# Softplus as one function, eight load buffers and column groups kept together in a four-layer convolution and state-space kernel

## The chip, the cores and the metric

The kernel runs on one core of a Trainium2 chip. The core has five engines with an instruction queue each, worked off in order: TensorE (PE; its weight loads are shown apart as PEld), VectorE (DVE), ScalarE (ACT), GpSimd (POOL) and SyncE (SP), which here only issues DMAs. The metric is the device time of one execution in microseconds. All data are float32.

## The reference

Eight images of 384 channels and 32 x 32 pixels go through four layers. Layer 0 is a two-way selective state-space layer (Mamba) beside a small convolution, layer 1 a block with a depthwise convolution, linear attention and an MLP, layer 2 a sum of large depthwise convolutions, layer 3 a pointwise and a 13 x 13 depthwise convolution with GELU. The change touches layer 0 and, through a shared helper, layer 1. Of layer 0, for a sequence of 1024 pixels in either direction:

```python
u = silu(causal_conv4(u) + conv1d_b)
dt, Bm, Cm = split(u @ x_proj_w.T, [24, 40])
delta = softplus(dt @ dt_proj_w.T + dt_proj_b)
h = exp(delta * A) * h + (delta * u) * Bm      # per channel and each of 16 states, step by step
y = sum(h * Cm over the 16 states) + u * D
y = y * silu(z)
```

## The kernel before

The program is written with a tile framework: the author writes operations on tiles from pools with a fixed number of buffers, in a trace order; a scheduler then orders each engine's instructions by priority (earlier in the trace first) and by its own estimate of when inputs and buffers are ready, and the program with its semaphore waits is fixed from there on. Each engine's order is that of the built program.

**Stages.** `_layers01` runs the `front` of image 0 alone, then for each image b the state recurrence `scan(b)`, into which it deals out pieces of `front(b + 1)` and of `layer1(b - 1)` by quotas; in the first scan a weight folding, and later the preparation of the large convolutions' kernels, run beside it. After the last scan come the rest of `layer1(7)` and the large convolutions of layers 2 and 3, which the change leaves alone.

**The scan.** 12 units (direction, half of the sequence, block of 128 channels) of 4 rounds each. A round does 4 of the 16 states: a tile's 128 partitions hold 32 channels x 4 states, and two tiles `hs` of 1024 columns hold the block's 128 channels. Per tile: ACT makes `da`, the exponential of delta times A, in two halves (L776); DVE multiplies delta u with B (`du`, L781) and runs two scans (L793); POOL multiplies with C (L802). The function `sums` (L732), two rounds later, adds the four states of each channel on PE: four products, each with a 32-column selection matrix `selt`, write to the four 32-partition strips of one PSUM tile `acc` (L736). There are eight `hs` buffers and four `da` buffers. Delta and delta u come from DRAM through SP's queue into `rep` tiles (six buffers).

**Column groups.** The same form, products with 32 output columns at four places of the array, is in `col32` (L507 to L514, its product is L511): it does the depthwise 3 x 3 convolutions of layer 0 (`lc`) and layer 1 (`dw`), by `conv3`, with three taps, and the causal convolution (`c`, from the `ut` loads) with one. Each of its four strips reads a tile loaded from DRAM, tag `im`, six buffers. The projection `xd` (L652) has two groups of 64 columns.

**Softplus.** For each of three channel blocks and either direction, PE multiplies `dt` (L667) into PSUM; ACT makes softplus(a) as relu(a) + ln(1 + exp(-|a|)): Abs (L671) and Relu (L672) read PSUM with the bias, then Exp (L676) and Ln (L678) run on the first result. The addition is on DVE in `deltas` (L683), a piece that is put off by one step; it also forms delta u (L684) in the other temporary, sends both to DRAM by POOL's queue (L685, L686), adds u of both directions in the place of the first (L687) and scales it by D (L689). `t2` is the pool of 128 x 512 temporaries, eleven buffers; `uc` tiles are of the tag `a6`, seven buffers.

ACT evaluates functions from a table that holds a set of them; ACT_TABLE_LOAD rows in the profile are the exchanges of that set.

Of the kernel before, what the change touches and what calls it, by code (L numbers as in the profile page):

```python
# [1 line left out]

# [7 lines left out]
AF = mybir.ActivationFunctionType  # L10
# [6 lines left out]
NC = C // P  # L17
H = 32
W = 32
L = H * W  # L20
HALF = 512
# [12 lines left out]
NR = NST // 4  # L34
IMG = (H + 2) * (W + 2)

N_A6, N_T2, N_S2, N_W, N_IM = 7, 11, 3, 4, 6
N_REP, N_DA, N_HS = 6, 4, 8
TP = H * (KP // 2)
PADW = KS // 2  # L40
HIMG = H // 2 * (W + 2)
# [333 lines left out]
def _layers01(tc, nc, B, xv, x2_d, dram, ident, mean_w, eps5, eps6, one, half, minus1, vec, bns, bnt,  # L375
# [12 lines left out]
    with ExitStack() as ctx:  # L388
# [26 lines left out]
        dlv = dl_d.rearrange("b d (c p) l -> b d p c l", p=P)  # L415
        vv = v_d.rearrange("b d (c p) l -> b d p c l", p=P)
# [7 lines left out]
        wx = const(xproj_t.rearrange("(k p) e -> p k e", p=P), [P, NC, 64], "wx")  # L424
# [9 lines left out]
        selt = const(sel, [P, 32], "selt")  # L434
# [27 lines left out]
        def t2(name):  # L462
            return sp.tile([P, HALF], FP, tag="t2", name=name, bufs=N_T2)
# [17 lines left out]
        late = []  # L481
# [22 lines left out]
                    start=(k == 0), stop=(k == NC - 1),  # L504
                )

        def col32(ps, lhs, rhs, taps):  # L507

            for i in range(taps):
                for j in range(4):  # L510
                    nc.tensor.matmul(  # L511
                        ps[32 * j : 32 * j + 32, :], lhs(j, i), rhs(j, i),
                        start=(i == 0), stop=(i == taps - 1), skip_group_check=True,
                    )  # L514

        def rows(t):
            return t.rearrange("p (h w) -> p h w", w=W)
# [13 lines left out]

        def conv3(t_d, slot, h, c, taps, name, psum=psum):

            ims = []
            for j in range(4):
                im = sp.tile([P, 18 * (W + 2)], FP, tag="im", name=f"{name}_i{j}", bufs=N_IM)
                src = bass.AP(
                    t_d.tensor, t_d[slot, 32 * (4 * c + j), 16 * h * (W + 2)].offset,
                    [[IMG, 32], [1, 3], [1, 18 * (W + 2) - 2]],
                )  # L540
                nc.sync.dma_start(im[:96, 0 : 18 * (W + 2) - 2], src)
                ims.append(im.rearrange("p (h w) -> p h w", w=W + 2))
            ps = psum(name)
            col32(
                ps, lambda j, i: taps[:96, (4 * c + j) * 3 + i, :],
                lambda j, i: ims[j][:96, i : i + 16, 0:W], 3,
            )
            return ps

# [22 lines left out]
        def front(b):  # L572

            xn = []
            for h in range(2):
# [7 lines left out]
                t, mid = image6(f"xn_{b}_{h}")  # L583
# [42 lines left out]
            for h in range(2):  # L626
                cols = bass.ts(h, HALF)
                ucs = [a6(f"uc_{b}_{h}_{d}") for d in range(2)]
                for c in range(NC):
                    uts = []  # L630
                    for j in range(4):
                        ut = sp.tile([P, 18 * (W + 2)], FP, tag="im", name=f"ut_{b}_{h}_{c}_{j}", bufs=N_IM)
                        src = bass.AP(
                            u_d.tensor, u_d[b % 2, 32 * (4 * c + j), h * HALF].offset,
                            [[UL, 32], [1, 4], [1, HALF + 3]],
                        )
                        nc.sync.dma_start(ut[:, 0 : HALF + 3], src)
                        uts.append(ut)
                    for d in range(2):
                        ps = psum(f"c1_{b}_{h}_{c}_{d}")  # L640
                        col32(
                            ps, lambda j, i: t1[:, d * NG + 4 * c + j, :],
                            lambda j, i: uts[j][:, 3 * d : 3 * d + HALF], 1,
                        )
                        nc.scalar.activation(ucs[d][:, c, :], ps, AF.Silu, bias=vec("conv1d_b", c))
                    yield 2

                xd = t2(f"xd_{b}_{h}")
                ps = psum(f"xd_{b}_{h}")
                for k in range(NC):  # L650
                    for d in range(2):
                        nc.tensor.matmul(  # L652
                            ps[64 * d : 64 * d + 64, :], wx[:, k, :], ucs[d][:, k, :],
                            start=(k == 0), stop=(k == NC - 1), skip_group_check=True,
                        )
                nc.scalar.copy(xd, ps)
                for d in range(2):
                    lo = 64 * d + DTR
                    nc.scalar.dma_start(bc_d[b, d][:, cols], xd[lo : lo + 2 * NST, :])
                yield 3  # L660

                for c in range(NC):
                    dls, ts = [], []
                    for d in range(2):
                        ps = psum(f"dt_{b}_{h}_{d}_{c}")
                        at = slice(64 * d, 64 * d + DTR)
                        nc.tensor.matmul(  # L667
                            ps, wdt[at, c * P : (c + 1) * P], xd[at, :], start=True, stop=True
                        )
                        t, dl = t2(f"sp_{b}_{h}_{d}_{c}"), t2(f"dl_{b}_{h}_{d}_{c}")  # L670
                        nc.scalar.activation(t, ps, AF.Abs, bias=vec("dt_b", c))  # L671
                        nc.scalar.activation(dl, ps, AF.Relu, bias=vec("dt_b", c))  # L672
                        ts.append(t)
                        dls.append(dl)
                    for t in ts:
                        nc.scalar.activation(t, t, AF.Exp, scale=-1.0)  # L676
                    for t in ts:
                        nc.scalar.activation(t, t, AF.Ln, bias=one)  # L678

                    def deltas(h=h, c=c, dls=dls, ts=ts, ucs=ucs):  # L680
                        for d in range(2):
                            dl, t = dls[d], ts[d]
                            nc.vector.tensor_add(dl, dl, t)  # L683
                            nc.vector.tensor_mul(t, dl, ucs[d][:, c, :])  # L684
                            nc.gpsimd.dma_start(dlv[b, d][:, c, bass.ts(h, HALF)], dl)  # L685
                            nc.gpsimd.dma_start(vv[b, d][:, c, bass.ts(h, HALF)], t)  # L686
                        nc.vector.tensor_add(ucs[0][:, c, :], ucs[0][:, c, :], ucs[1][:, c, :])  # L687
                        ud = t2(f"ud_{b}_{h}_{c}")
                        nc.scalar.activation(ud, ucs[0][:, c, :], AF.Copy, scale=vec("D", c))  # L689
                        nc.scalar.dma_start(udv[b][:, c, bass.ts(h, HALF)], ud)  # L690

                    defer(1, deltas)
                    yield 3

        def scan(b):
# [5 lines left out]
            late = []  # L701
# [27 lines left out]
                    ts.append(t)  # L729
                return ts  # L730

            def sums(k, r, hs, acc, y0, zt):  # L732
                d, h, c = units[k]
                cols = bass.ts(h, HALF)
                for j in range(4):
                    nc.tensor.matmul(  # L736
                        acc[32 * j : 32 * j + 32, :], selt, hs[j // 2][:, bass.ts(j % 2, HALF)],
                        start=(r == 0), stop=(r == NR - 1), skip_group_check=True,
                    )
                if r == 0:  # L740
                    nc.tensor.matmul(acc, ident, y0, start=False, stop=False, skip_group_check=True)
                if r < NR - 1:
                    return
                if d == 0:
                    yt = s2(f"yt_{b}_{h}_{c}")
                    nc.scalar.copy(yt, acc)
                    nc.scalar.dma_start(yfv[b][:, c, cols], yt)
                else:
                    nc.vector.tensor_mul(zt, acc, zt)
                    nc.gpsimd.dma_start(gv[b][:, c, cols], zt)  # L750
# [3 lines left out]
            acc = y0 = zt = nxt = None  # L754
            for k, (d, h, c) in enumerate(units):
                cols = bass.ts(h, HALF)
                second = k % (2 * NC) >= NC
                for r in range(NR):
                    if r == 0:
                        acc = accp.tile([P, HALF], FP, tag="acc", name=f"acc_{b}_{d}_{h}_{c}")  # L760
                        y0 = s2(f"y0_{b}_{d}_{h}_{c}")
# [3 lines left out]
                        nc.sync.dma_start(zt, zv[b][:, c, cols])  # L765
                    if r == 1 and k + 1 < len(units):
                        nxt = [load(k + 1, 0)]
                    hs = []
                    way = slice(None) if d == 0 else slice(None, None, -1)
                    end = HALF - 1 if d == 0 else 0  # L770
                    for i in range(2):
# [25 lines left out]
                        if not second:  # L797
# [4 lines left out]
                        nc.gpsimd.tensor_mul(  # L802
                            pairs(t), pairs(t), bct[r][:, 1:2, :].to_broadcast([P, 2, HALF])
                        )
                        hs.append(t)
                    late.append((k, r, hs, acc, y0, zt))
# [407 lines left out]
```

## Time and profile before

| | us |
|---|---|
| median of 10 runs | 5787.8 (5779.2 to 5796.4) |
| the profiled execution | 5790.1, span 5788.3 |
| front of image 0, alone | 0 to 215 |
| eight scans with what is dealt into them | 215 to 4630 |
| rest of layer 1 for image 7 | 4630 to about 4980 |
| large convolutions | about 4980 to 5788 |
| busy: PE / DVE / ACT / POOL | 4819 / 3676 / 3065 / 2898 |
| of ACT: 776 table loads of 1283 ns | 996 |

The mean granted clock of TensorE is 0.897 of full speed; in the first scan it is 0.70. Busy times are shares of stages with different limits, so they are read by stage. In the rows of groups, the count and the mean of one instruction stand first, then the idle time of the engine just before it and what ended it. A product in float32 leaves two records on PE.

### The profile page before, as it was taken

To read this page: it belongs to the slowest core of one execution; us is meant where nothing else is said; L and a number is where in the kernel's file an instruction comes from. 1 tells how busy PE (TensorE), PEld (TensorE's weight loads), DVE (VectorE), ACT (ScalarE), POOL (GpSimd) and SP (SyncE) were. 2 spreads that over 40 slices of the span, in tenths; PEclk is the share of its full clock that TensorE was granted. 3 is DMA by queue.
4 is the path that set the end of the run, shared out by engine and by line. 5 is a ranking of instruction groups with operands and counts; after the bars stand their busy time and mean duration, and the time that the engine had idled before them with its cause. 6 is when DMAs were issued, how large, how long until landed. Compare 5 with 4: busy or idle time off the path is not lost. (4 is left out here: it accounts for less than half of the span.)

```text
span 5788.3 us, 57844 instructions
## 1 busy us (share of the span) xinstructions
PE 4819.3 (83%) x19550; PEld 2105.0 (36%) x19550; DVE 3676.0 (64%) x3775; ACT 3064.8 (53%) x4116; POOL 2898.2 (50%) x1603
## 2 busy tenths in 40 slices
PE   5576579977988799879988997899778869899999
PEld 1121124322332243223323332333233324598498
DVE  0399997868687768786878786878678801011211
ACT  1656546774567567846784687468645613000211
POOL 3276676557554656564656564656466700110133
PEclk7677689988999899889998998999889979999999
DMA  9555475677567756764566467546644541366676
GB/s 299 187 183 174 144 251 186 229 194 217 187 210 202 216 171 192 166 208 133 186 206 191 140 177 191 186 140 178 180 143 131 127 95 49 91 170 158 194 166 150
DMA packets 528255, 1012.16 MB, mean 175 GB/s; under 512 B 60616, under 2 KB 196248, under 8 KB 527960
## 3 DMA queue, kind: packets, MB, share of 16 engines
q1 hardware_dynamic: 387952, 665.99, 38.1%
q0 software_dynamic: 71136, 248.53, 16.4%
q10 hardware_dynamic: 68872, 93.95, 5.2%
q8 instruction: 155, 2.54, 0.2%
q14 instruction: 140, 1.15, 0.1%
HBM read 763.86 MB, written 288.36 MB: 182 GB/s over the span
## 5 line engine op out<-in xcount | busy, mean ns | idle before, releaser
L802 POOL TENSOR_TENSOR hs<-hs,bct 128x1024 f32<-128x1024 f32 x768 | 2380.7, 3101 | 1171.1 <-DVE hs L793 662.2
L776 ACT ACTIVATE da<-dlt,neg_a 128x512 f32<-128x512 f32 x1536 | 1032.4, 714 | 849.0 <-DVE hs L793 761.3
L793 DVE TENSOR_TENSOR_SCAN hs<-da,carry,du 128x512 f32<-128x512 f32 x768 | 947.0, 1268 | 449.5 <-PE acc L736 213.0
L781 DVE TENSOR_TENSOR du<-vr,bct 128x1024 f32<-128x1024 f32 x768 | 1044.7, 1360 | 41.3 <-issue 16.6
L793 DVE TENSOR_TENSOR_SCAN hs<-da,du 128x512 f32<-128x512 f32 x768 | 901.2, 1208 | 153.3 <-ACT da L776 73.6
L736 PE MATMUL acc<-hs,selt 128*32 128x512 f32 x3072 | 737.8, 675 | 300.5 <-POOL hs L802 247.5
L1064 PE MATMUL mo<-hm,w 128*128 128x512 f32 x1152 | 566.2, 632 | 82.4 <-ACT hm L1062 61.3
L502 PE MATMUL mf<-ln,w 128*128 128x512 f32 x1152 | 543.3, 612 | 33.3 <-ACT dl L672 32.3
L736 PEld LDWEIGHTS acc<-hs,selt 128*32 128x32 f32 x3072 | 124.8, 115 | 727.5 <-POOL hs L802 395.7
L1064 PEld LDWEIGHTS mo<-hm,w 128*128 128x128 f32 x1152 | 215.9, 198 | 427.5 <-issue 257.0
L776 ACT ACT_TABLE_LOAD x265 | 340.0, 1283 | 38.1 <-DVE hs L793 26.1
L502 PEld LDWEIGHTS mf<-ln,w 128*128 128x128 f32 x1152 | 214.2, 194 | 346.5 <-issue 284.3
L316 PE MATMUL cv_b<-xt_b,toep 128*64 128x256 f32 x2688 | 304.8, 388 | 14.1 <-DVE xt_b L298 14.1
L316 PE MATMUL cv_a<-xt_a,toep 128*64 128x256 f32 x2688 | 305.8, 389 | 9.1 <-DVE xt_a L298 9.1
L502 PE MATMUL in<-xn,win 128*128 128x512 f32 x576 | 292.6, 640 | 22.8 <-ACT phi_k L874 21.9
L511 PE MATMUL dw<-dw_i,t3b 96*32 96x512 f32 x1152 | 234.9, 718 | 81.3 <-DMA dw_i<-h_d 81.3
L316 PEld LDWEIGHTS cv_b<-xt_b,toep 128*64 128x64 f32 x2688 | 282.5, 199 | 36.7 <-issue 16.3
L316 PEld LDWEIGHTS cv_a<-xt_a,toep 128*64 128x64 f32 x2688 | 282.8, 199 | 31.7 <-issue 11.3
L511 PE MATMUL lc<-lc_i,t 96*32 96x512 f32 x1152 | 224.6, 685 | 52.5 <-issue 28.6
L511 PE MATMUL c<-ut,t 128*32 128x512 f32 x768 | 193.6, 677 | 50.5 <-DMA ut<-u_d 38.8
L502 PE MATMUL op<-g,wo 128*128 128x512 f32 x288 | 143.4, 649 | 81.1 <-DMA g<-g_d 54.9
L1062 ACT ACTIVATE hm<-mf,biasf 128x512 f32<-128x512 f32 x192 | 130.6, 687 | 146.6 <-PE mf L502 145.0
(189 smaller groups left out, 5635.1 us busy)
## 6 DMA issues: line engine op xcount, KB each, us to landing
dlt<-dl_d SPq DMA_DIRECT2D x384, 256.0 KB, 4.4
vr<-v_d SPq DMA_DIRECT2D x384, 256.0 KB, 4.6
bct<-bc_d SPq DMA_DIRECT2D x256, 256.0 KB, 4.1
ut<-u_d SPq DMA_DIRECT2D x192, 257.5 KB, 4.9
lc_i<-xn_d SPq DMA_DIRECT2D x192, 228.8 KB, 4.8
dw_i<-h_d SPq DMA_DIRECT2D x192, 228.8 KB, 4.1
tp_d<-g_d POOLq DMA_DIRECT2D x64, 672.0 KB, 7.7
w<-w_d SPq DMA_DIRECT2D x64, 576.0 KB, 5.6
```

The costliest lines, as they stand in the source:

```text
L316: nc.tensor.matmul(ps[2 * H * e : 2 * H * (e + 1), 0:BW], tp[:, 2 * (g % (GB // 2)) + e, :, :, t].rearrange("p c j -> p (c j)"), rhs, star ...
L502: nc.tensor.matmul(ps, w[:, k, m * P : (m + 1) * P], rhs[k] if isinstance(rhs, list) else rhs[:, k, :], start=(k == 0), stop=(k == NC - 1),)
L511: nc.tensor.matmul(ps[32 * j : 32 * j + 32, :], lhs(j, i), rhs(j, i), start=(i == 0), stop=(i == taps - 1), skip_group_check=True,)
L736: nc.tensor.matmul(acc[32 * j : 32 * j + 32, :], selt, hs[j // 2][:, bass.ts(j % 2, HALF)], start=(r == 0), stop=(r == NR - 1), skip_group ...
L776: nc.scalar.activation(da[:, bass.ts(j, HALF)], dlt[:, bass.ts(j, HALF)], AF.Exp, scale=neg_a[:, g, r : r + 1],)
L781: nc.vector.tensor_mul(pairs(du), pairs(vt), bct[r][:, 0:1, :].to_broadcast([P, 2, HALF]),)
L793: nc.vector.tensor_tensor_scan(t[:, s][:, way], da[:, s][:, way], du[:, s][:, way], k_c if second else 0.0, ALU.mult, ALU.add,)
L802: nc.gpsimd.tensor_mul(pairs(t), pairs(t), bct[r][:, 1:2, :].to_broadcast([P, 2, HALF]))
L1062: nc.scalar.activation(hm, ps, AF.Gelu, bias=biasf[:, NC * i + f, :])
L1064: nc.tensor.matmul(acc[m], wb[:, f, m * P : (m + 1) * P], hm, start=(i == 0 and f == 0), stop=(i == FF // C - 1 and f == NC - 1),)
```

## The change

Three things:

- Softplus is one activation on ACT, from PSUM with the bias, into `dl`; Abs, Relu, Exp, Ln and DVE's addition go.
- `t2` has nine buffers, `im` has eight. Delta u is written over u in `uc` (and sent from there), the sum of both directions is formed first, in a `t2` tile of its own.
- A helper `together` takes a list of products. The first gets a scheduling edge without a semaphore behind all that makes their inputs (`made`: the loads, the last Silu, or POOL's two products); the others follow at raised priority and in program order. It is used for `col32`, for `xd` and for the four products of `sums`.

```diff
-N_A6, N_T2, N_S2, N_W, N_IM = 7, 11, 3, 4, 6
+N_A6, N_T2, N_S2, N_W, N_IM = 7, 9, 3, 4, 8
+AHEAD = 5000
...
-        def col32(ps, lhs, rhs, taps):
-            for i in range(taps):
-                for j in range(4):
-                    nc.tensor.matmul(
-                        ps[32 * j : 32 * j + 32, :], lhs(j, i), rhs(j, i),
-                        start=(i == 0), stop=(i == taps - 1), skip_group_check=True,
-                    )
+        behind = mybir.DependencyInfo(mybir.DependencyClass.NoSync, mybir.DependencyReason.DATA)
+
+        def together(products, made):
+            for i, product in enumerate(products):
+                if i == 0:
+                    first = product()
+                    for m in made:
+                        tc.add_manual_dep(first.ins, m.ins.name, behind, reason="together")
+                else:
+                    with tc.high_priority(AHEAD):
+                        tc.keep_in_program_order(product())
+
+        def col32(ps, lhs, rhs, taps, made):
+            together([
+                partial(
+                    nc.tensor.matmul, ps[32 * j : 32 * j + 32, :], lhs(j, i), rhs(j, i),
+                    start=(i == 0), stop=(i == taps - 1), skip_group_check=True,
+                )
+                for i in range(taps) for j in range(4)
+            ], made)
...
-                        t, dl = t2(f"sp_{b}_{h}_{d}_{c}"), t2(f"dl_{b}_{h}_{d}_{c}")
-                        nc.scalar.activation(t, ps, AF.Abs, bias=vec("dt_b", c))
-                        nc.scalar.activation(dl, ps, AF.Relu, bias=vec("dt_b", c))
-                        ts.append(t)
+                        dl = t2(f"dl_{b}_{h}_{d}_{c}")
+                        nc.scalar.activation(dl, ps, AF.Softplus, bias=vec("dt_b", c))
                         dls.append(dl)
-                    for t in ts:
-                        nc.scalar.activation(t, t, AF.Exp, scale=-1.0)
-                    for t in ts:
-                        nc.scalar.activation(t, t, AF.Ln, bias=one)
...
+                        ud = t2(f"ud_{b}_{h}_{c}")
+                        nc.vector.tensor_add(ud, ucs[0][:, c, :], ucs[1][:, c, :])
                         for d in range(2):
-                            dl, t = dls[d], ts[d]
-                            nc.vector.tensor_add(dl, dl, t)
-                            nc.vector.tensor_mul(t, dl, ucs[d][:, c, :])
-                            nc.gpsimd.dma_start(dlv[b, d][:, c, bass.ts(h, HALF)], dl)
-                            nc.gpsimd.dma_start(vv[b, d][:, c, bass.ts(h, HALF)], t)
-                        nc.vector.tensor_add(ucs[0][:, c, :], ucs[0][:, c, :], ucs[1][:, c, :])
-                        ud = t2(f"ud_{b}_{h}_{c}")
-                        nc.scalar.activation(ud, ucs[0][:, c, :], AF.Copy, scale=vec("D", c))
+                            v = ucs[d][:, c, :]
+                            nc.vector.tensor_mul(v, dls[d], v)
+                            nc.gpsimd.dma_start(dlv[b, d][:, c, bass.ts(h, HALF)], dls[d])
+                            nc.gpsimd.dma_start(vv[b, d][:, c, bass.ts(h, HALF)], v)
+                        nc.scalar.activation(ud, ud, AF.Copy, scale=vec("D", c))
                         nc.scalar.dma_start(udv[b][:, c, bass.ts(h, HALF)], ud)
...
-                for j in range(4):
-                    nc.tensor.matmul(
-                        acc[32 * j : 32 * j + 32, :], selt, hs[j // 2][:, bass.ts(j % 2, HALF)],
+                together([
+                    partial(
+                        nc.tensor.matmul, acc[32 * j : 32 * j + 32, :], selt,
+                        hs[j // 2][:, bass.ts(j % 2, HALF)],
                         start=(r == 0), stop=(r == NR - 1), skip_group_check=True,
                     )
+                    for j in range(4)
+                ], made)
...
-                        nc.gpsimd.tensor_mul(
+                        made.append(nc.gpsimd.tensor_mul(
                             pairs(t), pairs(t), bct[r][:, 1:2, :].to_broadcast([P, 2, HALF])
-                        )
+                        ))
```

More of the change, by code (lines that the diff above doesn't have):

```diff
@@ L1 @@
 from contextlib import ExitStack
+from functools import partial
 import concourse.bass as bass
@@ L532, in conv3 @@
         def conv3(t_d, slot, h, c, taps, name, psum=psum):
-            ims = []
+            ims, made = [], []
             for j in range(4):
@@ L540, in conv3 @@
                 )
-                nc.sync.dma_start(im[:96, 0 : 18 * (W + 2) - 2], src)
+                made.append(nc.sync.dma_start(im[:96, 0 : 18 * (W + 2) - 2], src))
                 ims.append(im.rearrange("p (h w) -> p h w", w=W + 2))
@@ L545, in conv3 @@
                 ps, lambda j, i: taps[:96, (4 * c + j) * 3 + i, :],
-                lambda j, i: ims[j][:96, i : i + 16, 0:W], 3,
+                lambda j, i: ims[j][:96, i : i + 16, 0:W], 3, made,
             )
@@ L629, in front @@
                 for c in range(NC):
-                    uts = []
+                    uts, made = [], []
                     for j in range(4):
@@ L636, in front @@
                         )
-                        nc.sync.dma_start(ut[:, 0 : HALF + 3], src)
+                        made.append(nc.sync.dma_start(ut[:, 0 : HALF + 3], src))
                         uts.append(ut)
@@ L642, in front @@
                             ps, lambda j, i: t1[:, d * NG + 4 * c + j, :],
-                            lambda j, i: uts[j][:, 3 * d : 3 * d + HALF], 1,
+                            lambda j, i: uts[j][:, 3 * d : 3 * d + HALF], 1, made,
                         )
-                        nc.scalar.activation(ucs[d][:, c, :], ps, AF.Silu, bias=vec("conv1d_b", c))
+                        uc = nc.scalar.activation(
+                            ucs[d][:, c, :], ps, AF.Silu, bias=vec("conv1d_b", c)
+                        )
                     yield 2
@@ L649, in front @@
                 ps = psum(f"xd_{b}_{h}")
-                for k in range(NC):
-                    for d in range(2):
-                        nc.tensor.matmul(
-                            ps[64 * d : 64 * d + 64, :], wx[:, k, :], ucs[d][:, k, :],
-                            start=(k == 0), stop=(k == NC - 1), skip_group_check=True,
-                        )
+                together([
+                    partial(
+                        nc.tensor.matmul, ps[64 * d : 64 * d + 64, :], wx[:, k, :], ucs[d][:, k, :],
+                        start=(k == 0), stop=(k == NC - 1), skip_group_check=True,
+                    )
+                    for k in range(NC) for d in range(2)
+                ], [uc])
                 nc.scalar.copy(xd, ps)
@@ L662, in front @@
                 for c in range(NC):
-                    dls, ts = [], []
+                    dls = []
                     for d in range(2):
@@ L669, in front, with deltas @@
                         )
-                        t, dl = t2(f"sp_{b}_{h}_{d}_{c}"), t2(f"dl_{b}_{h}_{d}_{c}")
-                        nc.scalar.activation(t, ps, AF.Abs, bias=vec("dt_b", c))
-                        nc.scalar.activation(dl, ps, AF.Relu, bias=vec("dt_b", c))
-                        ts.append(t)
+                        dl = t2(f"dl_{b}_{h}_{d}_{c}")
+                        nc.scalar.activation(dl, ps, AF.Softplus, bias=vec("dt_b", c))
                         dls.append(dl)
-                    for t in ts:
-                        nc.scalar.activation(t, t, AF.Exp, scale=-1.0)
-                    for t in ts:
-                        nc.scalar.activation(t, t, AF.Ln, bias=one)
-                    def deltas(h=h, c=c, dls=dls, ts=ts, ucs=ucs):
-                        for d in range(2):
-                            dl, t = dls[d], ts[d]
-                            nc.vector.tensor_add(dl, dl, t)
-                            nc.vector.tensor_mul(t, dl, ucs[d][:, c, :])
-                            nc.gpsimd.dma_start(dlv[b, d][:, c, bass.ts(h, HALF)], dl)
-                            nc.gpsimd.dma_start(vv[b, d][:, c, bass.ts(h, HALF)], t)
-                        nc.vector.tensor_add(ucs[0][:, c, :], ucs[0][:, c, :], ucs[1][:, c, :])
-                        ud = t2(f"ud_{b}_{h}_{c}")
-                        nc.scalar.activation(ud, ucs[0][:, c, :], AF.Copy, scale=vec("D", c))
+                    def deltas(h=h, c=c, dls=dls, ucs=ucs):
+                        ud = t2(f"ud_{b}_{h}_{c}")
+                        nc.vector.tensor_add(ud, ucs[0][:, c, :], ucs[1][:, c, :])
+                        for d in range(2):
+                            v = ucs[d][:, c, :]
[3 more added lines that the diff above has]
+                        nc.scalar.activation(ud, ud, AF.Copy, scale=vec("D", c))
                         nc.scalar.dma_start(udv[b][:, c, bass.ts(h, HALF)], ud)
@@ L730, in load, with sums @@
                 return ts
-            def sums(k, r, hs, acc, y0, zt):
+            def sums(k, r, hs, made, acc, y0, zt):
                 d, h, c = units[k]
                 cols = bass.ts(h, HALF)
-                for j in range(4):
-                    nc.tensor.matmul(
-                        acc[32 * j : 32 * j + 32, :], selt, hs[j // 2][:, bass.ts(j % 2, HALF)],
+                together([
+                    partial(
+                        nc.tensor.matmul, acc[32 * j : 32 * j + 32, :], selt,
+                        hs[j // 2][:, bass.ts(j % 2, HALF)],
                         start=(r == 0), stop=(r == NR - 1), skip_group_check=True,
                     )
+                    for j in range(4)
+                ], made)
                 if r == 0:
@@ L767, in scan @@
                         nxt = [load(k + 1, 0)]
-                    hs = []
+                    hs, made = [], []
                     way = slice(None) if d == 0 else slice(None, None, -1)
@@ L801, in scan @@
                             )
-                        nc.gpsimd.tensor_mul(
+                        made.append(nc.gpsimd.tensor_mul(
                             pairs(t), pairs(t), bct[r][:, 1:2, :].to_broadcast([P, 2, HALF])
-                        )
+                        ))
                         hs.append(t)
-                    late.append((k, r, hs, acc, y0, zt))
+                    late.append((k, r, hs, made, acc, y0, zt))
                     if c == NC - 1 and k + 1 < len(units) and r > 0:
```

## The prediction

> **What bounds the kernel now.** I read the table by stage first, then the waits of the stages, then the groups of instructions. The eight scans run from 215 to 4630 us; ahead of them stands the front of image 0, behind them the rest of layer 1 for image 7 and the large convolutions. Three rows by stage (columns: us, then busy time of PE, PEld, DVE, ACT and POOL, granted clock, DMA):
>
> ```profile
> 215.00:724.00 509.00, 314.73 (x988) 85.04 (x988) 431.94 (x416) 312.46 (x421) 325.88 (x151) 0.70 0.50 166
> 2442.00:3012.00 570.00, 490.40 (x1720) 179.07 (x1717) 439.78 (x435) 379.25 (x496) 330.28 (x156) 0.92 0.58 177
> 4145.00:4630.00 485.00, 396.23 (x1288) 148.52 (x1292) 400.21 (x396) 259.93 (x355) 315.34 (x127) 0.90 0.49 137
> ```
>
> The first scan has only the next front beside it: DVE is busy 432 of 509 us and PE 315, so DVE sets it. A scan in the middle has a front and a layer 1 beside it: DVE does the same work (440), PE goes to 490, ACT to 379, and the stage takes 61 us more. No engine is full; what is added is engines waiting for each other in their fixed orders. The waits, by who waited for whom:
>
> ```profile
> ACT da L776 <- DVE hs L793: 761.3, 340, 19.5
> PEld acc L736 <- POOL hs L802: 395.7, 151, 9.2
> DVE hs L793 <- PE acc L736: 257.3, 51, 22.1
> DVE hs L793 <- ACT da L776: 255.0, 83, 14.0
> PE acc L736 <- POOL hs L802: 247.5, 100, 7.6
> DVE dl L683 <- ACT sp L678: 97.3, 30, 24.6
> ```
>
> It is a ring. DVE's scans stand 257 us for PE (the state tile is free only when the sums of L736 have read it) and 255 us for ACT's decay factors; ACT's 761 us before those factors cost nothing, as they wait for DVE to hand tiles back.
>
> **Softplus (L671 to L683).** The groups that go, with busy time and mean ns, and one that stays, L645, with the operands that Softplus has (PSUM in, a pointer as bias):
>
> ```profile
> L671 ACT ACTIVATE sp<-dt,pk 128x512 f32<-128x512 f32 x96 | 65.4, 682 | 99.9 <-PE dt L667 74.7 <-DMA dl_d<-dl 15.5 <-DMA ud_d<-ud 9.6
> L645 ACT ACTIVATE uc<-c,pk 128x512 f32<-128x512 f32 x96 | 65.4, 687 | 91.0 <-PE c L511 71.5 <-PE acc L736 18.6
> L672 ACT ACTIVATE dl<-dt,pk 128x512 f32<-128x512 f32 x96 | 65.4, 681 | 1.4 <-DMA bct<-bc_d 1.3 <-DMA v_d<-sp 0.2
> L678 ACT ACTIVATE sp<-sp,one 128x512 f32<-128x512 f32 x96 | 65.4, 716 | 0.7
> L676 ACT ACTIVATE sp<-sp 128x512 f32<-128x512 f32 x96 | 57.2, 628 | 0.4
> ...
> L683 DVE TENSOR_TENSOR dl<-dl,sp 128x512 f32<-128x512 f32 x96 | 100.3, 1068 | 97.3 <-ACT sp L678 97.3
> ```
>
> ACT loses 65.4 + 65.4 + 57.2 + 65.4 = 253.4 us and gains 96 Softplus. No row has one; the nearest ends are L672 (681 ns) and L678 (716), and I take L645's 687: 66 us. Net -187 us of busy time, 7/8 of it (-164) inside the scans.
>
> The loads of ACT's function table are the catch. Abs and Relu ran under whichever table stood; Softplus has one of its own. Counted in the order of the built programs the loads are 776 before and 777 after: Softplus brings 65, and Ln's fall from 107 to 48. At 1283 ns a load (the rows of ACT_TABLE_LOAD) that is +1.3 us.
>
> The Trainium skill ("ScalarE: Activation LUTs", What ACT_TABLE_LOAD costs) puts a switch at about 2.66 us, load and drain together, where this trace has 1283 ns rows with the next activation right behind. By that figure as by the row, one more load is nothing.
>
> DVE loses L683: 96 x 1068 ns = 100 us, 84 of them (90 us) beside scans. The product with u (L684, 767 ns) and the sum of both directions (L687, 950 ns) stay, writing elsewhere: +0. DVE is busy 78% of a middle scan; I put that share on the path: **-70 us**. The rest of the 90 uncovers waits that were already running.
>
> DVE's wait for ACT is 255.0 + 97.3 = 352 us, which bounds the gain of a shorter ACT; the other end is +0, if the waits move to DVE's own inputs. A pair of chunks held ACT for 2 x (682 + 681 + 628 + 716) = 5.4 us besides loads and now 1.4. Since da waits for DVE far longer than the reverse, I take a seventh: **-50 us**.
>
> **Column groups as one (L511, L736).** Four products on 32 columns run beside each other if nothing stands between them:
>
> ```profile
> 2051.42 1.04 PE L736 MATMUL acc<-hs,selt 128*32 128x512 f32 x2
> 2052.40 0.93 PE L957 MATMUL kvs<-kp,vt 128*97 128x96 f32 x8
> ...
> 2059.09 1.06 PE L736 MATMUL acc<-hs,selt 128*32 128x512 f32 x6
> ```
>
> Two records are one product: one alone takes 1.04 us, three together 1.06. A burst therefore costs about 0.98 us (2051.42 to 2052.40) whatever it holds. Counting bursts in program order: acc 508 to 399 (384 would be whole), lc 169 to 144, depthwise dw 174 to 162, c 119 to 100: 165 bursts fewer. Changes between products of different column widths fall from 1107 to 961. A product of 128 columns takes 0.87 us (28 records in 12.12 us), so a change costs about 0.11: 165 x 0.87 + 146 x 0.11 = 160 us less for PE.
>
> The Trainium skill ("TensorEngine Tiling (Array Packing)", Key Properties) says that changing the tiling mode drains TensorE; the 0.11 us agrees.
>
> By the starts of the records, acc really ran in some 660 bursts: another 150 were broken by an input that came late. The new first product stands behind all four inputs in the plan, but no semaphore is added for it, so such breaks can go or stay. What it can give on the path is bounded by DVE's waits on acc, 257.3 (L793) plus 45.5 (L749): 303 us; the other end is a loss, priced below. PE does not set the first scan, and the broken pieces often ran while PE waited for POOL anyway. I take a sixth: **-50 us**.
>
> **Eight load buffers, nine t2 tiles, delta u in u's place.** SP stood for the convolutions to free a load buffer (its queue's waits):
>
> ```profile
> SPq L541 <- PE lc L511: 213.0, 47, 18.8
> SPq L541 <- PE dw L511: 147.4, 63, 8.3
> SPq L637 <- PE c L511: 135.6, 45, 28.8
> ```
>
> With eight, a whole second set of four is in flight. Inside the scans a load queued behind these has the slack of the scan's six prefetch tiles: 0. Where nothing else runs, it counts: the front of image 0 has six lc convolutions one after another at 8 to 16 us each (L615 runs at 106.55, 116.13, 132.53, 141.12, 150.68, 166.48 us), and image 7 six dw ones at about 8 us with 5 to 6 us of PE each. At 2 us each that is 24; with some of it covered by DMA (share 0.85 in the front): **-20 us**, between 0 and -45.
>
> t2 falls from 11 to 9, but a chunk needs three instead of five: 0. The product delta u now leaves from u's own tile, so that tile waits for its store (4.6 us to landing); 16 pairs of tiles, each followed by other work on a pool of seven: 0, at most 16 x 4.6 = 74 us if every one stood. The stores on POOL's and ACT's queues keep number and size, and each waits for DVE as before, with the POOL multiplications of L802 behind it on POOL.
>
> **Sum.** -70 -50 -50 -20 = -190. The profiled execution took 5790.1 us (span 5788.3), 2.3 us over the median of ten, 5787.8. So **5600**.
>
> **Rivals.** (1) *PE stands at the head of its queue (slower).* A group kept as one blocks everything behind it until POOL has written the second state tile; one POOL multiplication is 3.1 us (2380.7 us over 768). The 643 us that L736 already waits for POOL speak for it; against it, the plan now puts other products ahead until the last input is due. It decides where more than 190/3.1 = 61 of 384 groups stand one multiplication longer with DVE waiting behind; at 95 groups, 295 - 190 = +105 us: 5895. (2) *The work goes but the stage does not move.* ACT and PE are off the path in that only POOL and DVE's own chain matter: just half of DVE's 90, and the ends: about 5735, and near zero if u's tile costs something. (3) *PE's breaks at run time vanish too.* Then DVE's waits on acc and on ACT mostly go; the middle scans, 570 us on average, come most of the way to the first scan's 509 less its 13 of L683: six times some 60 of those 74 us, plus the ends: 5400. (4) *Softplus holds PSUM longer.* Before, Abs could empty PSUM at once; now a table load of 1.28 us may stand ahead while PE waits for one of two buffers: 65 x 1.28 = 83 us if all were exposed: with the rest of the sum, 5683.
>
> The Trainium skill ("ScalarE: Activation LUTs", Table sets: the hidden batching unit) speaks for rival 4: cheap functions sit in every set and a function with its own set is to be batched, which a Softplus per chunk is not. The trace agrees so far as Abs and Relu needed no load.
>
> **Chances.** The sum 0.55 (own range 5500 to 5690), rival 4 at 0.10, rival 2 at 0.15 (a third of it within 0.2%), rival 3 at 0.07, rival 1 at 0.13. Differences under 0.2% (12 us) can't be told from none. Faster: 0.55 + 0.10 + 0.10 + 0.07 = 0.82; same 0.05; slower 0.13. The range from 5440 to 5790 leaves out most of rivals 1 and 3.
>
> **What would show it.** The profile after should have no L683 add, ACT busy near 2880 and PE's column-group products at least 150 us less busy; DVE's waits on acc and da smaller; middle scans near 545 us; the last 1150 us about unchanged. I am wrong if DVE's wait for acc grows, if PE's wait for POOL grows beyond 643, or if the scans keep their length with ACT 187 us emptier.

## The result, and the profile after

The changed kernel takes 5604.0 us (median; 5583.4 to 5611.8), the kernel before 5789.2 in the same comparison: a ratio of 0.968, with a 95% interval of 0.967 to 0.969. The profiled execution has a span of 5581.6 us; it was the shortest of its kernel, so the traces lie 207 us apart where the medians lie 185 apart.

By stage (columns as before: us, busy time of PE, PEld, DVE, ACT and POOL, granted clock, DMA), the first scan, a middle one and the last one. The boundaries are moved with the scans, which now begin at 198 us and end at 4440 (before, the last operation of the scans ended at 4627):

```profile
198.00:676.00 478.00, 303.27 (x962) 81.44 (x958) 424.09 (x405) 286.72 (x370) 332.93 (x157) 0.66 0.53 176
2331.00:2874.00 543.00, 446.24 (x1667) 169.12 (x1664) 433.52 (x417) 332.74 (x438) 326.61 (x151) 0.90 0.59 179
3968.00:4440.00 472.00, 404.04 (x1353) 154.40 (x1351) 408.10 (x396) 280.88 (x374) 317.64 (x133) 0.93 0.52 148
```

The front of image 0 is 17 us shorter (215 to 198), the time behind the last scan 19 us (1161 to 1142), and the eight scans take the rest of the 207 us between the two spans. The middle scan went from 570 to 543 us. PE is 44 us less busy in it and ACT 47, but DVE only 6. Of the whole kernel (busy us by engine):

```profile
PE 4643.6 (83%) x19550; PEld 2078.0 (37%) x19550; DVE 3652.0 (65%) x3679; ACT 2891.8 (52%) x3829; POOL 2896.2 (52%) x1603
```

ACT lost 173 us, PE 176, DVE 24, though 100 us of DVE's additions went. The waits that answer to those of before:

```profile
PEld acc L521 <- POOL hs L817: 233.8, 81, 6.9
DVE hs L808 <- ACT da L791: 227.9, 81, 8.3
DVE hs L808 <- PE acc L521: 154.5, 37, 14.6
PEld acc L516 <- POOL hs L817: 143.2, 77, 8.3
PE acc L521 <- POOL hs L817: 140.5, 68, 5.4
...
PE acc L516 <- POOL hs L817: 71.4, 29, 6.6
...
DVE uc L698 <- ACT dl L690: 22.8, 2, 21.7
```

DVE's scans wait 103 us less for the sums (257 to 154.5); their wait for the decay factors fell by 27 (255 to 228), that for the delta chain from 97 to 23. The 643 us that PE stood for POOL are 589 (the four rows of `acc`). From this trace alone the groups kept together look like the main gain: of DVE's waits, the one for the sums fell most. The experiments say otherwise.

### The profile page after: what moved, and what is told of

The parts are those of the page before. It is cut to its first block, busy times and chain, and to the rows that moved or that the text cites. A ratio compares the mean times of both kernels' runs of the same rounds, so it can differ in the third digit from the quotient of the medians.

```text
span 5581.6 us, 57337 instructions
## 1 busy us (share of the span) xinstructions
PE 4643.6 (83%) x19550; PEld 2078.0 (37%) x19550; DVE 3652.0 (65%) x3679; ACT 2891.8 (52%) x3829; POOL 2896.2 (52%) x1603
## 5 line engine op out<-in xcount | busy, mean ns | idle before, releaser
L817 POOL TENSOR_TENSOR hs<-hs,bct 128x1024 f32<-128x1024 f32 x768 | 2385.8, 3108 | 1133.9 <-DVE hs L808 546.8
L796 DVE TENSOR_TENSOR du<-vr,bct 128x1024 f32<-128x1024 f32 x768 | 1052.6, 1371 | 50.0 <-DMA vr<-v_d 34.7
L521 PE MATMUL acc<-hs,selt 128*32 128x512 f32 x2304 | 584.7, 672 | 140.6 <-POOL hs L817 140.5
L504 PE MATMUL mf<-ln,w 128*128 128x512 f32 x1152 | 561.4, 629 | 62.2 <-ACT uc L662 45.3
L516 PE MATMUL acc<-hs,selt 128*32 128x512 f32 x768 | 438.3, 664 | 112.6 <-POOL hs L817 71.4
L300 DVE COPY xt_b<-xt_b 64x2480 f32<-64x2480 f32 x24 | 39.3, 1638 | 261.7 <-DMA xt_b<-xp_d 249.0
L516 PEld LDWEIGHTS acc<-hs,selt 128*32 128x32 f32 x768 | 64.8, 114 | 371.3 <-issue 214.9
L521 PE MATMUL dw<-dw_i,t3b 96*32 96x512 f32 x1056 | 197.8, 623 | 3.5 <-DMA dw_i<-h_d 3.3
```

Source lines behind the costliest of these rows:

```text
L300: nc.vector.tensor_copy(half1[:, :, 0 : XL - 1], half0[:, :, 1:XL])
L504: nc.tensor.matmul(ps, w[:, k, m * P : (m + 1) * P], rhs[k] if isinstance(rhs, list) else rhs[:, k, :], start=(k == 0), stop=(k == NC - 1),)
L516: first = product()
L521: tc.keep_in_program_order(product())
L796: nc.vector.tensor_mul(pairs(du), pairs(vt), bct[r][:, 0:1, :].to_broadcast([P, 2, HALF]),)
L817: made.append(nc.gpsimd.tensor_mul(pairs(t), pairs(t), bct[r][:, 1:2, :].to_broadcast([P, 2, HALF])))
```

## The experiments

The chips differ by half a per cent (the kernel before took 5757 to 5761 us in these runs), so each kernel is compared by its ratio to the kernel before on the same chip. All ratios together, with 95% intervals:

| Softplus | load buffers | kept together | ratio |
|---|---|---|---|
| yes | 6 | no | 0.985 (0.983 to 0.987) |
| no | 8 | no | 0.983 (0.981 to 0.985) |
| no | 6 | all | 1.011 (1.009 to 1.013) |
| yes | 6 | all | 0.991 (0.990 to 0.993) |
| yes | 8 | no | 0.964 (0.962 to 0.966) |
| yes | 8 | all (the changed kernel) | 0.968 (0.965 to 0.970) |
| yes | 8 | convolutions, projection | 0.964 (0.961 to 0.966) |
| yes | 8 | sums | 0.963 (0.960 to 0.966) |

One more thing differs: the first row keeps delta u in a t2 tile of its own, with eleven t2 tiles. The other rows with Softplus have delta u in u's place and nine tiles.

### Softplus alone

```diff
-                        nc.scalar.activation(t, ps, AF.Abs, bias=vec("dt_b", c))
-                        nc.scalar.activation(dl, ps, AF.Relu, bias=vec("dt_b", c))
+                        nc.scalar.activation(dl, ps, AF.Softplus, bias=vec("dt_b", c))
...
-                    for t in ts:
-                        nc.scalar.activation(t, t, AF.Exp, scale=-1.0)
-                    for t in ts:
-                        nc.scalar.activation(t, t, AF.Ln, bias=one)
...
-                            nc.vector.tensor_add(dl, dl, t)
                             nc.vector.tensor_mul(t, dl, ucs[d][:, c, :])
```

> The kernel before with Softplus alone: Abs, Relu, Exp, Ln and DVE's addition go; delta u gets a t2 tile of its own, six load buffers, eleven t2 tiles, products in their old order. By the prediction's sum (DVE's addition 70, DVE's wait for ACT 50) 120 us faster, ratio 0.979, with DVE's wait for the delta chain (97 us) nearly gone and DVE some 90 us less busy in the scans. Rival: DVE's busy time hardly falls, as it did in the changed kernel (3676 to 3652), and Softplus is worth only 50 to 70 us, ratio 0.988 to 0.991, the groups being the larger part.

Measured 0.985: 1.5%, some 87 us by the ratio, between the two expectations. DVE's busy time fell by 62 us (3676.0 to 3613.5), more than in the changed kernel. Its waits for ACT fell by 118 us, from 255.0 + 97.3 to 213.1 + 21.1:

```profile
DVE hs L786 <- ACT da L769: 213.1, 74, 18.3
DVE sp L677 <- ACT dl L671: 21.1, 4, 19.5
```

Not all of this reached the kernel's time, because other waits came in its place: DVE's wait for the loads of `vr` and `bct`, for one, rose from 14 to 65 us. With eight load buffers Softplus gave 1.9% (0.983 to 0.964), but there it came with delta u in u's place.

### The groups alone

The whole of the helper and its three uses on the old Softplus, with `N_T2, N_IM = 11, 6`.

> The kernel before with the column groups kept together alone: old Softplus, six load buffers, eleven t2 tiles. Bursts in program order fall from 970 to 838. By the prediction's sum 50 us faster, ratio 0.991, DVE's wait for the sums (257 us at the scan) falling by about that. Rival: the groups carry the change, 110 us or more, ratio 0.981 or less, with DVE's wait for the sums down by 100 us as in the changed kernel.

Measured 1.011: slower by 1.1%. Both expectations fell, and DVE's wait for the sums did not fall with the bursts (267.8 us after 257.3). PE's busy time did go down, by 72 us (4819.3 to 4747.1).

### Six load buffers again

```diff
-N_A6, N_T2, N_S2, N_W, N_IM = 7, 9, 3, 4, 8
+N_A6, N_T2, N_S2, N_W, N_IM = 7, 9, 3, 4, 6
```

> The changed kernel with six load buffers again (nine t2 tiles, all else as changed). By the prediction's sum it gives back 20 us, at the ends: front of image 0 back from 198 to about 210 us, the last 1142 us longer by some 8; ratio to the kernel before 0.971. Rival: loads queued on SP behind the convolutions' also hold up the scans, and it gives back 50 us or more, ratio 0.977 or above.

Measured 0.991: two buffers are worth 2.3%, some 134 us. That is the rival's size, but the traces do not show its mechanism: the waits of DVE, ACT and POOL for the scans' own loads (rows that name `dlt`, `vr` or `bct`) come to 110 us with six buffers and 108 with eight. The ends give 33 us (the front of image 0 ends at 215 us again). The rest is in the scans. The products that read the loads, in this kernel and then in the changed one (L516 is the first product of a group, L521 the others; the idle time and its causes stand last):

```profile
L521 PE MATMUL dw<-dw_i,t3b 96*32 96x512 f32 x1056 | 251.8, 750 | 47.3 <-DMA dw_i<-h_d 47.0
L521 PE MATMUL lc<-lc_i,t 96*32 96x512 f32 x1056 | 187.7, 677 | 30.8 <-DMA lc_i<-xn_d 30.8
L521 PE MATMUL c<-ut,t 128*32 128x512 f32 x576 | 166.3, 672 | 47.5 <-DMA ut<-u_d 47.3
...
L516 PE MATMUL dw<-dw_i,t3b 96*32 96x512 f32 x96 | 60.4, 717 | 23.9 <-DMA dw_i<-h_d 23.9
```

```profile
L521 PE MATMUL dw<-dw_i,t3b 96*32 96x512 f32 x1056 | 197.8, 623 | 3.5 <-DMA dw_i<-h_d 3.3
L521 PE MATMUL lc<-lc_i,t 96*32 96x512 f32 x1056 | 175.3, 663 | 10.4 <-DMA lc_i<-xn_d 10.2
L521 PE MATMUL c<-ut,t 128*32 128x512 f32 x576 | 121.2, 655 | 8.0 <-DMA ut<-u_d 8.0
...
L516 PE MATMUL dw<-dw_i,t3b 96*32 96x512 f32 x96 | 55.6, 664 | 32.7 <-DMA dw_i<-h_d 32.7
```

With six, a set of four has two loads in flight and two that can only start when the set before gives its buffers back; PE has begun the set and stands at the head of its queue: 149 us, against 58 with eight (3.4 us of it at the first lc products, not shown). The broken bursts show as PE's busy time: 666 us in these four rows against 550, and 84 us over the whole kernel (4727.2 to 4643.6). DVE's wait for the sums, which I had taken as the groups' own, goes with it:

```profile
DVE hs L808 <- PE acc L521: 251.2, 41, 22.4
DVE hs L808 <- ACT da L791: 224.0, 70, 13.0
```

It is 251 us with six buffers and 154.5 with eight, the groups being kept together in both; the wait for the decay factors is the same (224 and 228). That PE's standing is what DVE waits for is read from these waits and was not tried by itself.

### Eight load buffers on the kernel before

`N_T2, N_IM = 9, 8` in the kernel before, nothing else.

> The kernel before with eight load buffers and nine t2 tiles alone; old Softplus with its five t2 tiles a chunk, products in their old order. Theory after the first four runs: the two more buffers are worth some 120 us because PE stands at the head of its queue for a convolution's third and fourth load (144 us of PE's idle time in the kernel before, and DVE's scans stand behind it for the sums); then ratio 0.978 to 0.982, with PE's waits for dw, c and lc loads falling from 144 to under 70 us and DVE's wait for the sums from 258 towards 190. Rival: eight buffers pay only because Softplus left t2 tiles free; with five a chunk from a pool of nine ACT and DVE wait for t2 tiles, ratio 0.99 to 1.01.

Measured 0.983, 99 us faster: the theory held, at its weak end. The row of the kernel before that it rests on, and DVE's waits with eight:

```profile
L511 PE MATMUL dw<-dw_i,t3b 96*32 96x512 f32 x1152 | 234.9, 718 | 81.3 <-DMA dw_i<-h_d 81.3
```

```profile
DVE hs L793 <- PE acc L736: 210.4, 61, 12.8
DVE hs L793 <- ACT da L776: 183.2, 76, 12.0
```

With c (38.8) and lc (23.7) PE's waits for these loads were 144 us before; with eight buffers they are 46.1 + 9.5 + 8.5 = 64. DVE's wait for the sums fell from 257 to 210 us and its wait for the decay factors more, from 255 to 183, so the gain reaches DVE by both. Nine t2 tiles, with five of them in a chunk, did not eat it up: ACT's waits for the stores of delta, delta u and the scaled sum went from 69 to 80 us. So the buffers did not need Softplus.

### The products apart, and each use alone

The helper's loop replaced in the changed kernel:

```diff
-            for i, product in enumerate(products):
-                if i == 0:
-                    first = product()
-                    for m in made:
-                        tc.add_manual_dep(first.ins, m.ins.name, behind, reason="together")
-                else:
-                    with tc.high_priority(AHEAD):
-                        tc.keep_in_program_order(product())
+            for product in products:
+                product()
```

> The changed kernel with the products in their old way, without the edge and the priority; Softplus, eight load buffers and nine t2 tiles stay. Bursts in program order rise from 805 to 930. By the prediction's sum 50 us come back, ratio to the kernel before 0.977. Rival (groups carry the change): 100 us or more come back, ratio 0.986 or above.

Measured 0.964: nothing came back, the kernel is 0.4% faster than the changed one. The next three put the changed kernel beside itself with one of the two uses undone (the sums, or the convolutions and the projection, as plain loops).

> The changed kernel itself, beside the two kernels that undo one use of the helper each, so that they share the runs of the kernel before. Expected ratio 0.968, as measured first; if the groups kept together really cost time, it lies above the ratio of the kernel with the products apart, 0.9638.

> The changed kernel with the four products of the sums in their old way; the convolutions and the projection stay together. Bursts in program order 910, of them acc 494. Theory: keeping the sums together is what costs, because a group that stands for POOL's second tile blocks what is behind it; then this is as fast as all apart, ratio 0.962 to 0.965. Rival: the convolutions' groups cost (they stand for four loads); then it stays at 0.968 or above.

> The changed kernel with the convolutions and the projection in their old way; the sums stay together. Bursts in program order 828, of them acc 390. Theory (the sums' groups cost): ratio 0.967 or above. Rival (the convolutions' groups cost): 0.964 or below. If both this and the kernel with the convolutions alone lie between, the difference is the luck of the order rather than one part.

Measured 0.968, 0.964 and 0.963. Either use alone neither costs nor gains; both together lie 0.4% above. Neither theory on which part costs holds. What happens to PE can be read from the page: the spans and busy times of the kernel apart, then of the changed kernel:

```profile
span 5552.3 us, 57344 instructions
...
PE 4706.4 (85%) x19550; PEld 2074.9 (37%) x19550; DVE 3639.7 (66%) x3679; ACT 2894.8 (52%) x3832; POOL 2881.2 (52%) x1603
```

```profile
span 5570.4 us, 57337 instructions
...
PE 4641.7 (83%) x19550; PEld 2080.6 (37%) x19550; DVE 3647.2 (65%) x3679; ACT 2891.2 (52%) x3829; POOL 2896.7 (52%) x1603
```

Together, PE is 65 us less busy and idle for 929 us instead of 846: what it no longer spends on broken bursts it spends waiting, and more. The waits say on what: PE stands 588 us for POOL's products together and 500 apart. DVE's waits with the products apart:

```profile
DVE hs L802 <- PE acc L515: 192.8, 51, 11.5
DVE hs L802 <- ACT da L785: 176.1, 60, 16.9
```

Beside them the changed kernel (154.5 and 227.9) waits less for the sums and more for the decay factors. PE's wait for POOL does not set the price by itself: with the sums alone kept together it is 643 us, and that kernel is no slower.

One rival was not tried. The clock that TensorE was granted is lower wherever all groups are kept together: 0.882 to 0.888 beside 0.896 to 0.901 on the kernel before, 0.893 to 0.896 beside 0.901 to 0.907 with Softplus and six buffers, 0.895 to 0.899 beside 0.908 to 0.910 here; with either use alone it is 0.902 to 0.908. Whether the lower clock costs the time, or follows from the order, is open.

### Whole bursts by order alone

In the kernel with the products apart:

```diff
-                    for j in range(4)
+                    for j in (2, 3, 0, 1)
```

> The kernel with the products apart (ratio 0.9638), the four products of the sums taken in the order of strips 2, 3, 0, 1: the first then waits for POOL's second tile, and at run time none stands between the halves. No edge, no priority. Theory: bursts cost only PE time that the scans do not wait for; PE's busy time falls (below 4706 us), its idle time rises by as much, and the ratio stays between 0.960 and 0.967. Rival: whole bursts at run time, without the plan's edge, free PE where it is needed: ratio 0.958 or below with DVE's wait for the sums under 150 us.

Measured 0.969 (0.968 to 0.971), slower than that kernel by 0.55%. PE's busy time fell as expected (4706.4 to 4671.5) and its idle time rose by twice as much (846 to 914). The rival, that whole bursts free PE where it is needed, fell; the theory missed the size by two thousandths.

### The scaling by D put off

In the changed kernel ACT stood 133 us for DVE's sum of both directions, ahead of decay factors that DVE waits for (19 us before):

```profile
ACT ud L701 <- DVE ud L695: 133.1, 29, 9.8
```

```diff
-                        nc.scalar.activation(ud, ud, AF.Copy, scale=vec("D", c))
-                        nc.scalar.dma_start(udv[b][:, c, bass.ts(h, HALF)], ud)
+                        def scaled():
+                            nc.scalar.activation(ud, ud, AF.Copy, scale=vec("D", c))
+                            nc.scalar.dma_start(udv[b][:, c, bass.ts(h, HALF)], ud)
+
+                        defer(0, scaled)
```

> The kernel with the products apart (ratio 0.9638), ACT's scaling of the sum of both directions by D, and its store, put off by one more step. In the changed kernel ACT stands 133 us at the head of its queue for DVE's addition (19 us before the change), with decay factors behind it that DVE's scans wait for. Theory: that standing is on the path; ACT's wait for ud (86 us with the products apart) falls under 30, DVE's wait for ACT falls by 40 us or more, ratio 0.955 to 0.959. Rival: ACT has slack there (it waits 740 us for DVE before the decay factors), and the ratio stays at 0.961 to 0.966.

Measured 0.959 (0.957 to 0.961), the fastest kernel here, 5520.5 us. But not for the reason given: the wait did not go away. It is 97.6 us, after 85.7 in the kernel with the products apart, on which the edit was made.

```profile
ACT ud L697 <- DVE ud L689: 97.6, 26, 8.6
```

So the same edit was made on another order, the kernel with the sums alone kept together:

> The same putting-off of the scaling by D on another order: the changed kernel with only the sums kept together (ratio 0.963). If putting it off helps by itself, by whatever way, it gives the 0.5% again: 0.956 to 0.960. Rival: the gain of 0.5% was the luck of one order (ACT's wait for ud had not fallen, 98 us after 86); then this lies at 0.961 to 0.966 or on the other side.

Measured 0.971 (0.969 to 0.974): there it cost 0.8%. So the gain was the luck of one order and not the edit's own. (The granted clock goes with the time here too: 0.910 to 0.913 in the faster kernel, 0.901 to 0.902 in the slower.) This also sizes such luck: an edit that leaves the work alone moved this kernel by half a per cent to nearly one per cent either way, as the scheduler lays the whole program out anew.

### POOL's multiplication left out

In the changed kernel, L817 goes and the scans' results are summed without the multiplication by C; `made` holds the scans.

> The changed kernel without POOL's multiplication by C (left out; the scans' results are summed as they are). Theory on DVE's busy time, which fell by 24 us where 100 us of additions went: DVE's short operations run up to 2.8 us when they meet a POOL multiplication, and the first one after the scans meets it, whichever it is. Without POOL's multiplications the sum of both directions (mean 1638 ns), the carry copies (290) and the rest fall to their shortest times (0.67 us and 0.16 us), and DVE's busy time is some 300 us lower than 3652. Rival: the operations are slow for their own operands, and their means stay above 1 us and 250 ns.

One execution, 5262 us; what counts is the length of DVE's operations. The kernel before, the changed kernel, then the changed kernel without POOL's products:

```profile
L687 DVE TENSOR_TENSOR uc<-uc,uc 128x512 f32<-128x512 f32 x48 | 45.6, 950 | 0.1
```

```profile
L813 DVE COPY carry<-hs 128x2 f32<-128x2 f32 x384 | 111.4, 290 | 11.1
L695 DVE TENSOR_TENSOR ud<-uc,uc 128x512 f32<-128x512 f32 x48 | 78.1, 1638 | 2.6 <-ACT uc L662 1.8 <-DMA dl_d<-dl 0.8
```

```profile
L813 DVE COPY carry<-hs 128x2 f32<-128x2 f32 x384 | 69.8, 182 | 11.3
...
L695 DVE TENSOR_TENSOR ud<-uc,uc 128x512 f32<-128x512 f32 x48 | 32.1, 681 | 3.2 <-ACT uc L662 1.8 <-DMA dl_d<-dl 1.3
```

The theory held: the sum falls from 1638 to 681 ns, the carry copies from 290 to 182, and DVE as a whole from 3652.0 to 3374.9 us busy, 277 less. The largest part of that, 106 us, is the long multiplication of delta u by B (L796), which falls from 1371 to 1233 ns.

## Why the prediction was right, and where it was not

The total came out as forecast, 5604 against 5600, but partly by luck: the errors of its terms cancel. Term by term:

- **DVE's addition, 70 us.** The term that was mis-sized by its busy time: I subtracted the 100 us of L683 and kept everything else. DVE's busy time fell by 24 in the changed kernel and by 62 with Softplus alone. A third of L683's length was not its own: it ran some 0.68 us alone and up to 2.85 us when it met a POOL multiplication. Taken away in the changed kernel, it left the meeting to other operations: the sum of both directions went from 950 to 1638 ns, the carry copies from 211 to 290, the residual of L636 from 824 to 1120.
- **DVE's wait for ACT, 50 us.** The mechanism was right: 352 us (255.0 + 97.3) became 251 (227.9 + 22.8), three quarters of it the delta chain's own wait. The size cannot be read from that, as the buffers had a part in it. With Softplus alone the wait fell by 118 us and DVE's busy time by 62, and the kernel gained 87, where I had 120 for both terms. The two together were too large, and no run separates them.
- **The table loads, nothing.** Right: 777 against 776, L690 has 65 of them.
- **The column groups, 50 us.** The step that failed. The count agreed by luck: I forecast 160 us less of PE from the order of the groups and the page shows 176, but the groups make only 65 to 72 of it; the load buffers alone took 71 and Softplus alone 13. And PE's lost bursts were time in which it would have waited. The groups gave nothing in any of the three pairs of the table (+1.1%, +0.6%, where delta u's place differs too, and +0.4%). Whether they cost is open, as the last two lie within what an order's luck does, and each use alone measured no change. Rival 1 is thus neither shown nor refuted in its direction: PE's wait for POOL did not grow past 643 us, but beside the products apart it grew from 500 to 588.
- **Eight load buffers, 20 us, and nothing in the scans.** The step that failed the other way: 99 us on the kernel before and 134 in the changed one, of which the ends, where I had put all of it, give 33 in the changed one. I looked at what stands behind those loads on SP's queue, and not at what waits for them on PE. The row was in the page before (L511, dw, idle 81.3 us until its load); with c and lc it came to 144 us of PE at the head of its queue, with DVE's two waits behind it.
- **Rival 4, PSUM held longer,** did not happen as stated: the wait of PE's `mf` products for a PSUM buffer that a delta activation empties went from 32 to 17 us. Their wait for one that the Silu of `uc` empties went from 0.3 to 45, which no rival had. **Rival 2** (only half of the addition) was too low, as the load buffers pay. **Rival 3** took a fall of DVE's waits for granted that came to 40% for the sums and 11% for the decay factors.
- **Delta u in u's place, nine t2 tiles, 0.** Nine tiles did not eat up the buffers' gain on the kernel before. The place of delta u was not tried by itself.

## What to carry to other kernels

When one engine stands at the head of its queue for a load, ask what else that engine feeds: here 80 to 91 us less of PE's waiting for loads came with 99 to 134 us less of the kernel, while 65 to 72 us less of PE's busy time was worth nothing. Busy time that is saved on an engine which waits anyway turns into waiting, so price an edit by the waits that it ends, and ask which waits will take their place. And where a scheduler lays out the program, half a per cent between two versions is no evidence for a mechanism until the same edit has been made on a second order.

## What the runs showed of the hardware

A DVE operation on 128 x 512 elements with two operands in SBUF is stretched when it begins while a POOL multiplication (3.1 us) runs. Of the 96 additions of L683 in the kernel before, 23 began so and took 1.02 to 2.85 us each; six in which the addition began first, and 67 that met none, took 0.66 to 0.69. In the changed kernel 24 of the 48 sums of L695 began so (1.29 to 2.87 us), where of the 48 of L687 only six had. Without the multiplications L695 and L698 took at most 0.69 us. The carry copies, 0.17 us in the median, took up to 6.7 us with the multiplications and up to 0.87 without. DVE's scans, whose second operand lies in PSUM, keep their times in either case (1246 to 1284 ns with a carry).

The Trainium skill ("SBUF — State Buffer", Who interferes with whom) says that DVE and GpSimd share a pair of ports as an exclusive lock, that whoever issues first holds it for the whole instruction, and that a DVE instruction with two SBUF inputs contends with a GpSimd one that reads SBUF. For the operations with two SBUF inputs and for the scans the trace agrees (1.02 to 2.85 us against 0.66 to 0.69; the scans unchanged). An estimate by that rule would have priced the addition at its time alone, 96 x 0.68 = 65 us. Softplus alone took 62 from DVE, but the changed kernel only 24.
